# Layer 3's first product of the second-last quad moved among the last quad's norms, and the first quad worked out plainly ahead of the pairs

## The chip, the core and the metric

The kernel runs on one core of a Trainium2 chip. The metric is the device time of one execution in microseconds, the median of several runs; the kernel before takes 3154.85 us (three runs, 3150.97 to 3155.34). The profile is of one execution with a span of 3149.4 us. Engines are named as the profile names them: PE is TensorE's matmul side and PEld its weight loads, DVE is VectorE, ACT is ScalarE, POOL is GpSimd, SP is SyncE, which here only issues transfers.

## What is computed

Four residual graph layers with a layer norm after each, on x of shape 128 x 128 x 256 (graphs, nodes, features). Everything is float32.

```python
x = layernorm(x + L0(x))       # graph attention over 512 edges, 4 heads
x = layernorm(x + L1(x))       # three products by weights 256->512->1024->256, each mixed by adj*adj
x = layernorm(x + L2(x))       # three weights 256->256, mixed by diagonal, upper and lower part of adj
x = layernorm(x + L3(x))

def L3(features, A, W1, b1, g1, be1, W2, b2, g2, be2):
    A_hat = normalized(A + I)
    agg = einsum('nm,bmd->bnd', A_hat, features)
    h = relu(batchnorm(agg.reshape(-1, 256) @ W1.T + b1, g1, be1))   # 256 -> 512
    out = batchnorm(h @ W2.T + b2, g2, be2)                          # 512 -> 256
    return out
# batchnorm: mean and variance over ALL rows, that is, over all 128 graphs and 128 nodes
```

The two batch norms of layer 3 cut the computation in three. Nothing of the second product of layer 3 can begin before the first product has been done for every graph, and no output row is finished before the second product has been done for every graph.

## The kernel before

Graphs are handled in 32 quads of four, numbered 0 to 31. A first phase is a software pipeline: iteration k works on several quads at once, quad a = k - 1 in layers 2 and 3, quad c = k in layer 1, and later quads in layer 0. When a quad leaves it, two things have been stored to device memory: x3, the input of layer 3, and z, the first product of layer 3 (`hidden`), of which only the statistics are kept on the chip. The very last quad's z isn't stored: its norm's factors are known as soon as its statistics are, so it is normalized and passed through relu straight from PSUM (`hidden_last`).

The second phase loads z of all other quads, normalizes, applies relu, and multiplies by W2. The third phase adds x3 and does the last layer norm.

Many products are done two by two blocks at a time with seven block products in place of eight (class `Seven`, steps p1 to p7, with sums of blocks S1 to S4 of one operand and T1 to T4 of the other). The steps hang together through two PSUM banks y and z that are added to in turn:

```python
class Seven:
    def p1(self): self.y = ps("y"); self.mm(self.y, "A11", "B11", True);  self.k1 = self.part(self.y, 0)
    def p5(self): self.z = ps("z"); self.mm(self.z, "S1", "T1", True)
    def p2(self): x = ps("x");      self.mm(x, "A12", "B21", True);       self.out(0, 0, x, self.k1)
    def p6(self): self.mm(self.y, "S2", "T2", False);  self.k2 = self.part(self.y, 1)
    def p7(self): self.mm(self.y, "S3", "T3", False);  self.k3 = self.part(self.y, 2); self.out(1, 1, self.z, self.k3)
    def p4(self): self.mm(self.y, "A22", "T4", False); self.out(1, 0, self.y, None)
    def p3(self): self.mm(self.z, "S4", "B22", False); self.out(0, 1, self.z, self.k2)
# part: ScalarE copies the bank out.  out with a kept part: VectorE adds bank and part.
# out without one: ScalarE copies the bank.
```

The end of the first phase, for the last two quads:

```python
def stage_f(k):                       # agg, with A_hat, into SBUF
    pas = [ps("pa") for _ in range(DC)]
    for i0, dc in ((i0, dc) for i0 in range(0, QB, 2) for dc in range(DC)):
        for i in (i0, i0 + 1):
            nc.tensor.matmul(pas[dc][:, i * N:(i + 1) * N], s.xr[:, i, dc * P:(dc + 1) * P], ahat_t, ...)
    for dc, pa in enumerate(pas):
        nc.scalar.copy(ag[dc], pa)

def z_tile(k):                        # ONE buffer
    quads[k].zt = zpool.tile([P, K3, QB * N], F32, tag="z", name="z", bufs=1)

def hidden_stats(k):
    for c in range(K3):
        nc.vector.bn_stats(st1[:, c, k, :], zt[:, c, :])
    nc.sync.dma_start(z_dram[k], zt.rearrange("p c n -> p (c n)"))

def hidden_last(k, c):
    if c == 0:
        kept["z"] = z_tile(k)
    ...                               # two products 128x512 into ph
    nc.vector.bn_stats(st1[:, c, k, :], ph)
    batch_norm(st1, c, bn1, sc1, sh1, c)
    nc.scalar.activation(s.zt[:, c, :], ph, AF.Relu, bias=sh1[:, c:c + 1], scale=sc1[:, c:c + 1])

# iteration(31): a = 30, c = 31, nothing later
stage_f(30)
h = hidden(30, ...)
run(h.p1, h.p5); run(h.p2, h.p6); h.p7(); run(h.p4, h.p3)
hidden_stats(30)
for _ in third(31, 0): pass           # layer 1's third product, first two graphs
rest = third(31, 2); next(rest)
third_mix(31, 0); third_norm(31, 0)
for _ in rest: pass
third_mix(31, 2); third_norm(31, 2)
layer2(31, None): head(0), head(1), twelve of fourteen products
# iteration(32): a = 31
the rest of layer2(31): v.p4, v.p3, mixes, norms, store of x3
stage_f(31)
for i in range(K3): hidden_last(31, i)
```

The second phase takes quads in pairs, again with seven products, one pair's last two standing in the next pair. Two quads are left over and worked out plainly, with eight products of 128x512 each: quad 31, in front of the pairs, and quad 30, after them.

```python
nc.vector.tensor_add(s1, a21, a22)     # sums of W2's blocks: four of these
...
pairs = [begin(0)]                     # loads of z
for i in range(4): relus(pairs[0], i)
sums_of(pairs[0], 0)
plain(NQ - 1, load_z(NQ - 1), ...)     # quad 31, z is on the chip
for q in range(0, NQ - 2, 2):
    ...
    pair(pairs[d], pairs[d - 1] if d else None, next pair)
for c in range(K3): relu(z_last, c)
pair(None, pairs[-1], None)            # A22 product, then S4 product of the last pair
plain(NQ - 2, z_last, ..., True)       # quad 30, with the second batch norm in it
```

Of the kernel before, what the change touches and what calls it, by code (L numbers as in the profile page):

```python
# [8 lines left out]
F32 = mybir.dt.float32  # L9
# [17 lines left out]
def gnn_stack(ctx: ExitStack, tc: tile.TileContext, x, adj, w_qv_t, a, w_out_t, src, dst,  # L27
# [101 lines left out]
    with ExitStack() as phase:  # L129
# [76 lines left out]
            return t  # L206

        quads[0].xr = load_x(0)
        wqv = cload([P, DC, 2 * D], "wqv", w_qv_t.rearrange("(c p) f -> p c f", p=P))
        a_sb = cload([P, N], "adj", adj)  # L210
        a_bc = ctile([P, D], "a_bc", pool=cst)
        wt_t = ctile([P, N], "wt_t", pool=cst)
# [79 lines left out]

        def room_of(tag, n):

            t = {"m2": m2_tile, "adc": adc_tile}[tag]()
            return [t[:, i * 512:(i + 1) * 512] for i in range(n)]

        def queries(k, kept_at):
# [379 lines left out]
                s.xb = wk.tile([P, QB, D], F32, tag="xb", name=f"xb{k}", bufs=1)  # L678
            nc.gpsimd.tensor_add(s.xb[:, j:j + 2, :], xj, bias.unsqueeze(1).to_broadcast([P, 2, D]))  # L679

        def layer2(k, b):

            s = quads[k]
            adc = adc_tile()
            g = [wk.tile([P, 2, 3 * D], F32, tag="ms", name="g", bufs=1),
                 adc[:, :6 * D].rearrange("p (t f) -> p t f", t=2)]
            sums = [adc[:, 6 * D:], None]
            half = 3 * D // 2  # L690
# [91 lines left out]
            normed(1, mv)  # L782
            nc.sync.dma_start(x3_dram[k], s.xr.rearrange("p b d -> p (b d)"))

        def stage_f(k):

            s = quads[k]
            wide = wk.tile([P, DC, 3 * D], F32, tag="ms", name="ag", bufs=1)
            ag = [wide[:, i, :QB * N] for i in range(DC)]
            s.spare = [wide[:, i, QB * N:] for i in range(DC)]  # L790
            pas = [ps("pa") for _ in range(DC)]
            for i0, dc in ((i0, dc) for i0 in range(0, QB, 2) for dc in range(DC)):
                for i in (i0, i0 + 1):
                    nc.tensor.matmul(pas[dc][:, i * N:(i + 1) * N], s.xr[:, i, dc * P:(dc + 1) * P], ahat_t,
                                     start=True, stop=True)
            for dc, pa in enumerate(pas):
                nc.scalar.copy(ag[dc], pa)
            s.ag = ag

        def hidden_sums():  # L800

            blocks = {f"A{o + 1}{h + 1}": l3w1[:, h, o * 256:(o + 1) * 256] for o in range(2) for h in range(2)}
            for i in range(4):
                blocks[f"S{i + 1}"] = l3w1_s[:, i]
            sums_a(blocks, blocks)
            hidden.blocks = blocks

        def z_tile(k):
            quads[k].zt = zpool.tile([P, K3, QB * N], F32, tag="z", name="z", bufs=1)
# [73 lines left out]
        def run(*parts):  # L883
            for p in parts:
                p()

        def iteration(k):
# [5 lines left out]
                late_sums(c)  # L893
            parts = quads[a].layer2
            if not has_c:
                for _ in parts:
                    pass
            steps = softmax_parts(e) if has_e else iter(())
            if has_c:
                between = {i: [] for i in range(14)}  # L900
# [21 lines left out]
            if has_g:  # L922
                q = queries(g, room[:3])
            stage_f(a)
            if not has_c:
                for i in range(K3):
                    hidden_last(a, i)
                return
            h = hidden(a, room[5:] + room[2:4])
            if has_g:  # L930
# [25 lines left out]
                attention(e)  # L956
                scatter(e)
            rest = third(c, 2)
            if not has_b:
                next(rest)  # L960
                third_mix(c, 0)
                third_norm(c, 0)
                for _ in rest:
                    pass
                third_mix(c, 2)
                third_norm(c, 2)
                quads[c].layer2 = layer2(c, None)
                next(quads[c].layer2)
                next(quads[c].layer2)
                return  # L970
            mix1(b, 0)
            mix1(b, 2)
            third_mix(c, 0)
# [303 lines left out]
    with ExitStack() as phase:  # L1277
# [37 lines left out]
        with tc.manual_schedule(engines=None):  # L1315

            ws_ = ctile([P, 4, 2, P], "l3w2_s", pool=cst)
            a11, a12, a21, a22 = (w2t[:, 2 * h:2 * h + 2, o * P:(o + 1) * P] for o in range(2) for h in range(2))  # L1320
            s1, s2, s3, s4 = (ws_[:, i] for i in range(4))

# [8 lines left out]
            def plain(q, z, jobs, last=False):  # L1331
                ag = out_tile(q)
                po = [ps("po3") for _ in range(DC)]
                for o, c in jobs:
                    nc.tensor.matmul(po[o], w2t[:, c, o * P:(o + 1) * P], z[c // 2][:, c % 2, :],
                                     start=(c == 0), stop=(c == K3 - 1))
                for o in range(DC):
                    nc.vector.bn_stats(st2[:, o, q, :], po[o])
                    if last:
                        batch_norm(st2, o, bn2, sc2, sh2, K3 + o)  # L1340
                        halves(0, o, outs[0])
                        spread(o)
                    nc.vector.tensor_copy(ag[:, o, :], po[o])

            class Pair:
# [46 lines left out]
                    for c in (0, 1):  # L1392
                        relu(d.z[i % 2], 2 * (i // 2) + c)

            def pair(d, old, new):
# [12 lines left out]
                if d:  # L1408
                    sums_of(d, 3)
                    product(d.zb, s1, d.t[0], True)  # L1410
# [18 lines left out]
            nc.vector.tensor_add(s1, a21, a22)  # L1429
            nc.vector.tensor_sub(s2, s1, a11)  # L1430
            nc.vector.tensor_sub(s3, a11, a21)
            nc.vector.tensor_sub(s4, a12, s2)
            pairs = [begin(0)]
            for i in range(4):
                relus(pairs[0], i)
            sums_of(pairs[0], 0)

            plain(NQ - 1, load_z(NQ - 1), [(o, c) for c in range(K3) for o in range(DC)])
            for q in range(0, NQ - 2, 2):
                if q + 2 < NQ - 2:  # L1440
                    pairs.append(begin(q + 2))
                else:
                    z_last = load_z(NQ - 2)
                d, n = q // 2, len(pairs)
                pair(pairs[d], pairs[d - 1] if d else None, pairs[d + 1] if d + 1 < n else None)
            for c in range(K3):
                relu(z_last, c)
            pair(None, pairs[-1], None)
            plain(NQ - 2, z_last, [(o, c) for o in range(DC) for c in range(K3)], True)

            x3s, sums, mvs, coefs = {}, {}, {}, {}

# [123 lines left out]
```

## Time and profile before

| | |
|---|---|
| median of three runs | 3154.85 us |
| span of the profiled execution | 3149.4 us |
| busy: PE, PEld, DVE, ACT, POOL | 3077.0, 2403.3, 2306.6, 1376.0, 651.5 us |
| mean granted TensorE clock | 0.993 |
| moved by DMA | 340.04 MB, 108 GB/s over the span |
| first phase, up to quad 31's leaving it | to about 2825 us |
| batch norm and plain products of quad 31 | to about 2841 us |
| pairs | to about 3028 us |
| plain products of quad 30 and second batch norm | to about 3039 us |
| third phase | to the end |

How to read it: the busy time of PE over the whole span says little about this change, because the change touches only the place where one phase gives way to the next. There the engines run short of work and wait for one another, and the question is which wait ends last at each step. Three views answer it: busy time by stretches of time, the waits of PE within a stretch, and the timeline, which gives the start of each group of instructions and in brackets the idle time before it with what ended it. A product of this kernel shows as several records[...].

### The profile page before, as it was taken

The numbers are of one execution on the slowest core, as the hardware profiler recorded it, in microseconds if no ns is written. First come the engines' busy times: TensorE is split into PE (matmuls) and PEld (weight loads), VectorE is DVE, ScalarE is ACT, GpSimd is POOL, SyncE is SP. The second block draws the span as 40 slices with busy tenths as digits, with TensorE's granted clock in tenths as the row PEclk, the third lists the DMA queues.
The fourth block names the chain that finished last, engine by engine and source line by source line (L and its number), as shares of the span: only waits on it lengthen the run. The fifth ranks groups of instructions, "written<-read, shape, count | busy, mean of one in ns | idle before, by whom it ended". The sixth has DMA issues, their size and how long they took to land. (4 is left out here: it accounts for less than half of the span.)

```text
span 3149.4 us, 39744 instructions
## 1 busy us (share of the span) xinstructions
PE 3077.0 (98%) x14752; PEld 2403.3 (76%) x14752; DVE 2306.6 (73%) x4600; ACT 1376.0 (44%) x2548; POOL 651.5 (21%) x535
## 2 busy tenths in 40 slices
PE   7899999999999999999999999999999999989998
PEld 3678888888888888888888888888888887864444
DVE  7777777777777777777777777777777776447888
ACT  3344433444444444334344444444444344326668
POOL 2311222222121111122222211111122220001235
PEclk8999999999999999999999999999999999999999
DMA  5623333333333332333333333332333331005557
GB/s 179 160 68 88 101 108 97 106 108 108 101 86 103 104 91 79 98 108 101 101 108 108 103 94 92 107 91 76 97 108 101 101 108 41 21 31 195 173 195 275
DMA packets 117473, 340.04 MB, mean 108 GB/s; under 512 B 14881, under 2 KB 51617, under 8 KB 108961
## 3 DMA queue, kind: packets, MB, share of 16 engines
q0 software_dynamic: 44544, 147.88, 19.4%
q1 hardware_dynamic: 70976, 188.71, 17.0%
q8 instruction: 117, 1.92, 0.3%
q10 hardware_dynamic: 1760, 0.92, 0.1%
q14 instruction: 76, 0.61, 0.1%
HBM read 252.00 MB, written 85.46 MB: 107 GB/s over the span
## 5 line engine op out<-in xcount | busy, mean ns | idle before, releaser
L575 PE MATMUL ph<-m,w 128*128 128x256 f32 x2048 | 475.0, 380 | 0.0
L655 PE MATMUL p<-w,h 128*128 128x256 f32 x2048 | 463.8, 380 | 0.0
L575 PEld LDWEIGHTS ph<-m,w 128*128 128x128 f32 x2048 | 387.9, 191 | 78.4 <-issue 14.8
L655 PEld LDWEIGHTS p<-w,h 128*128 128x128 f32 x2048 | 389.7, 190 | 67.0 <-issue 8.1
L336 POOL DMA_INDIRECT zs<-qd,src_idx x120 | 117.2, 977 | 1347.8 <-DMA qd<-qt 1216.1
L575 PE MATMUL ph<-m,w_s 128*128 128x256 f32 x1536 | 357.5, 379 | 0.0
L575 PEld LDWEIGHTS ph<-m,w_s 128*128 128x128 f32 x1536 | 291.8, 190 | 52.9 <-issue 14.8
L336 POOL DMA_INDIRECT zs<-qd,dst_idx x120 | 188.1, 1568 | 352.5 <-DMA zs<-qd,src_idx 327.2
L581 ACT COPY u<-ph 128x512 f32<-128x512 f32 x128 | 74.8, 584 | 356.1 <-PE ph L575 356.1
L418 POOL DMA_INDIRECT attd<-at,att_idx x128 | 142.7, 1115 | 347.4 <-DMA attd<-at,att_idx 245.0
L591 ACT ACTIVATE h<-h 128x512 f32<-128x512 f32 x192 | 121.1, 630 | 135.6 <-DVE h L587 135.6
L113 ACT ACTIVATE ln_sd<-ln_mv,eps 128x2 f32<-128x2 f32 x192 | 55.9, 291 | 281.6 <-DVE ln_mv L108 277.8
L370 DVE TENSOR_TENSOR zs<-zs,a_bc 128x1024 f32<-128x1024 f32 x125 | 153.1, 1225 | 4.3
L371 DVE TENSOR_REDUCE scores<-zs 128x16 f32<-128x1024 f32 x125 | 152.5, 1220 | 4.3
L718 ACT COPY x2k<-y 128x384 f32<-128x384 f32 x192 | 92.0, 479 | 138.3 <-PE y L711 113.8
L368 DVE SCALAR_TENSOR_TENSOR zs<-zs 128x1024 f32<-128x1024 f32 x125 | 151.4, 1211 | 0.1
L106 DVE BATCH_NORM_STATS2 ln_st<-xr 128x6 f32<-128x256 f32 x384 | 144.5, 418 | 6.6
L121 DVE TENSOR_SCALAR xr<-xr,ln_mv,ln_rs 128x256 f32<-128x256 f32 x384 | 143.2, 415 | 7.0
L587 DVE TENSOR_TENSOR h<-ph,u 128x512 f32<-128x512 f32 x128 | 87.1, 680 | 73.1 <-PE ph L575 55.0
L437 ACT COPY adc<-ad 128x512 f32<-128x512 f32 x125 | 133.1, 1065 | 4.1 <-DMA ad<-attd 4.1
L679 POOL TENSOR_TENSOR xb<-xr,bias 128x512 f32<-128x512 f32 x64 | 99.3, 1551 | 160.0 <-DVE xr L121 150.7
L532 PE MATMUL pm<-wt_t,h 128*128 128x128 f32 x1024 | 126.7, 277 | 0.0
(342 smaller groups left out, 6071.1 us busy)
## 6 DMA issues: line engine op xcount, KB each, us to landing
ad<-attd SPq DMA_DIRECT2D x32, 1024.0 KB, 4.8
zd<-z SPq DMA_DIRECT2D x31, 1024.0 KB, 7.3
zl<-zd SPq DMA_DIRECT2D x62, 512.0 KB, 3.8
xr<-in_x_dram SPq DMA_DIRECT2D x32, 512.0 KB, 7.5
x3d<-xr SPq DMA_DIRECT2D x32, 512.0 KB, 2.6
x3l<-x3d SPq DMA_DIRECT2D x32, 512.0 KB, 5.1
out_dram<-x3l POOLq DMA_DIRECT2D x31, 512.0 KB
qd<-qt SPq DMA_DIRECT2D x30, 512.0 KB, 2.6
```

Source lines behind the costliest of these rows:

```text
L106: nc.vector.bn_stats(st[:, i, :], r[:, i, :])
L121: nc.vector.tensor_scalar(r[:, i, :], r[:, i, :], mv[:, i, 0:1], rs[:, i:i + 1], op0=ALU.subtract, op1=ALU.mult)
L336: nc.gpsimd.indirect_dma_start(out=s.z[c], out_offset=None, in_=s.qd, in_offset=bass.IndirectOffsetOnAxis(ap=idx[:, c:c + 1], axis=0), com ...
L368: nc.vector.scalar_tensor_tensor(z, z, SLOPE, z, op0=ALU.mult, op1=ALU.max)
L370: nc.vector.tensor_mul(z3, z3, a_bc.unsqueeze(1).to_broadcast([P, QB, D]))
L371: nc.vector.reduce_sum(s.es[:, c, :], z.rearrange("p (r d) -> p r d", d=DH), axis=AX.X)
L418: nc.gpsimd.indirect_dma_start(out=ad, out_offset=bass.IndirectOffsetOnAxis(ap=att_idx[:, c:c + 1], axis=0), in_=s.at[:, c, :], in_offset= ...
L437: (copy or nc.scalar.copy)(s.adc[:, j * H:(j + 1) * H, :], s.ad.rearrange("p (s r) -> p r s", r=R)[:, j * H:(j + 1) * H, :])
L532: nc.tensor.matmul(pm[:, c // 2, c % 2, :], quads[k].h1[i, c], wt_t, start=True, stop=True)
L575: nc.tensor.matmul(bank[g][:, i].rearrange("p b n -> p (b n)"), wa[:, c, f:f + P], s.m2[:, blk_b, c].rearrange("p b n -> p (b n)"), start= ...
L591: nc.scalar.activation(h, h if src_ is None else src_, AF.Relu)
L655: nc.tensor.matmul(p3[:, t * D:(t + 1) * D], s.h2[f // 2][:, f % 2, j + t, :], w3_sb[:, f, :], start=(f == 0), stop=(f == K2 - 1))
```

## The change

The first product of layer 3 for quad 30 is no longer done in one block ahead of quad 31's norms. Its seven steps are spread out: p1, p5 and p2 stand at the places where PE waited for the norms of layer 1 of quad 31, p6 and p7 among the products and norms of layer 2, p4 and p3 in the middle of `stage_f(31)`. The aim is that PE has a product to do while a norm runs on VectorE and ScalarE, and that the norms themselves begin earlier. To make room, the first half of layer 2's results for quad 31 is kept in the buffer m2 in place of ms, which still holds quad 30's aggregate. The sums of W2's blocks are made earlier too (`last_sums`), in the buffer that held layer 0's weights, which moves to another pool for that.

In the second phase the quad that is worked out plainly with stored z is quad 0 and no longer quad 30. Its products stand in front of the pairs, which now begin at quad 1 and end at quad 30. They are meant to give PE work while ScalarE and VectorE prepare the first pair. After the last pair there is now only that pair's end, with the S4 product ahead of the A22 product, and the second batch norm within it.

```diff
-        wqv = cload([P, DC, 2 * D], "wqv", ...)
+        wqv = cload([P, DC, 2 * D], "wqv", ..., pool=xpool)
...
-        def layer2(k, b):
+        def layer2(k, b, room=None):
...
-            g = [wk.tile([P, 2, 3 * D], F32, tag="ms", name="g", bufs=1),
+            g = [wk.tile([P, 2, 3 * D], F32, tag="ms", name="g", bufs=1) if room is None else room,
...
-        def stage_f(k):
+        def stage_f(k, amid=None):
...
+                if i0 and dc == 0 and amid:
+                    amid()
...
+        def last_sums():
+            kept["w2s"] = xpool.tile([P, 4, 2, P], F32, tag="wqv", name="l3w2_s", bufs=1)
+            ...
+            sums_a(a, {f"S{i + 1}": kept["w2s"][:, i] for i in range(4)})
...
 # iteration(32), a = 31
+                h = quads[a - 1].hidden
+                h.p6()
+                for _ in range(4):
+                    next(parts)
+                next(parts)
+                h.p7()
                 for _ in parts:
                     pass
+                def amid():
+                    run(h.p4, h.p3)
+                    hidden_stats(a - 1)
+                stage_f(a, amid)
+                for i in range(K3):
+                    hidden_last(a, i)
+                return
...
 # iteration(31), a = 30, c = 31
+                last_sums()
+                h = quads[a].hidden = hidden(a, room[5:] + room[3:5])
+                for _ in third(c, 0):
+                    pass
+                rest = third(c, 2)
+                next(rest)
+                third_mix(c, 0)
+                third_norm(c, 0)
+                for _ in rest:
+                    pass
+                h.p1()
+                third_mix(c, 2)
+                third_norm(c, 2)
+                lower = kept["m2"][:, :3 * 512].rearrange("p (t f) -> p t f", t=2)
+                quads[c].layer2 = layer2(c, None, lower)
+                next(quads[c].layer2)
+                run(h.p5, h.p2)
+                next(quads[c].layer2)
                 return
...
 # second phase
+            def finish(d):
+                product(d.zb, s4, d.b22, False)
+                result(d, 0, 1, d.zb, d.u2)
+                product(d.y, a22, d.t[3], False)
+                norm_over(0)
+                nc.vector.bn_stats(st2[:, 1, d.q, :], d.y)
+                norm_over(1)
+                nc.scalar.copy(outs[d.q][:, 1, :], d.y)
...
-            pairs = [begin(0)]
+            z_first = load_z(0)
+            pairs = [begin(1)]
+            for _ in plain(NQ - 1, load_z(NQ - 1)):
+                pass
+            for c in range(K3):
+                relu(z_first, c)
+            first_quad = plain(0, z_first)
+            next(first_quad)                    # the products; statistics and copies later, in the first pair
             for i in range(4):
                 relus(pairs[0], i)
-            sums_of(pairs[0], 0)
-            plain(NQ - 1, load_z(NQ - 1), ...)
-            for q in range(0, NQ - 2, 2):
+                if i == 1:
+                    sums_of(pairs[0], 0)
+            for q in range(1, NQ - 1, 2):
...
-            for c in range(K3):
-                relu(z_last, c)
-            pair(None, pairs[-1], None)
-            plain(NQ - 2, z_last, ..., True)
+            finish(pairs[-1])
```

More of the change, by code (lines that the diff above doesn't have):

```diff
@@ L208, in gnn_stack @@
         quads[0].xr = load_x(0)
[L209 removed]
+        wqv = cload([P, DC, 2 * D], "wqv", w_qv_t.rearrange("(c p) f -> p c f", p=P), pool=xpool)
         a_sb = cload([P, N], "adj", adj)
@@ L293, in room_of @@
         def room_of(tag, n):
-            t = {"m2": m2_tile, "adc": adc_tile}[tag]()
+            t = kept[tag] = {"m2": m2_tile, "adc": adc_tile}[tag]()
             return [t[:, i * 512:(i + 1) * 512] for i in range(n)]
@@ L806, in hidden_sums @@
             hidden.blocks = blocks
+        def last_sums():
+            kept["w2s"] = xpool.tile([P, 4, 2, P], F32, tag="wqv", name="l3w2_s", bufs=1)
+            a = {f"A{o + 1}{h + 1}": kept["w2t"][:, 2 * h:2 * h + 2, o * P:(o + 1) * P] for o in range(2)
+                 for h in range(2)}
+            sums_a(a, {f"S{i + 1}": kept["w2s"][:, i] for i in range(4)})
         def z_tile(k):
@@ L924, in iteration @@
             stage_f(a)
-            if not has_c:
-                for i in range(K3):
-                    hidden_last(a, i)
+            if not has_b:
+                last_sums()
[16 more added lines that the diff above has]
+                next(quads[c].layer2)
                 return
@@ L958, in iteration @@
             rest = third(c, 2)
[L959 to L970, printed above, removed]
             mix1(b, 0)
@@ L1315, in gnn_stack @@
         with tc.manual_schedule(engines=None):
-            ws_ = ctile([P, 4, 2, P], "l3w2_s", pool=cst)
+            ws_ = kept["w2s"]
             a11, a12, a21, a22 = (w2t[:, 2 * h:2 * h + 2, o * P:(o + 1) * P] for o in range(2) for h in range(2))
@@ L1329, in out_tile, with plain @@
                 return outs[q]
-            def plain(q, z, jobs, last=False):
+            def plain(q, z):
                 ag = out_tile(q)
                 po = [ps("po3") for _ in range(DC)]
-                for o, c in jobs:
+                for o, c in ((o, c) for c in range(K3) for o in range(DC)):
                     nc.tensor.matmul(po[o], w2t[:, c, o * P:(o + 1) * P], z[c // 2][:, c % 2, :],
                                      start=(c == 0), stop=(c == K3 - 1))
+                yield
                 for o in range(DC):
                     nc.vector.bn_stats(st2[:, o, q, :], po[o])
[L1339 to L1342, printed above, removed]
                     nc.vector.tensor_copy(ag[:, o, :], po[o])
@@ L1393, in relus, with pair @@
                         relu(d.z[i % 2], 2 * (i // 2) + c)
-            def pair(d, old, new):
+            def pair(d, old, new, rest=()):
                 if d:
@@ L1409, in pair @@
                     sums_of(d, 3)
+                    for _ in rest:
+                        pass
                     product(d.zb, s1, d.t[0], True)
@@ L1427, in pair, with norm_over @@
                     relus(new, 3)
[L1429 to L1432, printed above, removed]
-            pairs = [begin(0)]
+            def norm_over(o):
+                batch_norm(st2, o, bn2, sc2, sh2, K3 + o)
+                halves(0, o, outs[0])
+                spread(o)
+            def finish(d):
[9 more added lines that the diff above has]
+            for _ in plain(NQ - 1, load_z(NQ - 1)):
+                pass
+            for c in range(K3):
+                relu(z_first, c)
+            first_quad = plain(0, z_first)
+            next(first_quad)
             for i in range(4):
                 relus(pairs[0], i)
-            sums_of(pairs[0], 0)
-            plain(NQ - 1, load_z(NQ - 1), [(o, c) for c in range(K3) for o in range(DC)])
-            for q in range(0, NQ - 2, 2):
-                if q + 2 < NQ - 2:
+                if i == 1:
+                    sums_of(pairs[0], 0)
+            for q in range(1, NQ - 1, 2):
+                if q + 2 < NQ - 1:
                     pairs.append(begin(q + 2))
-                else:
-                    z_last = load_z(NQ - 2)
                 d, n = q // 2, len(pairs)
-                pair(pairs[d], pairs[d - 1] if d else None, pairs[d + 1] if d + 1 < n else None)
-            for c in range(K3):
-                relu(z_last, c)
-            pair(None, pairs[-1], None)
-            plain(NQ - 2, z_last, [(o, c) for o in range(DC) for c in range(K3)], True)
+                pair(pairs[d], pairs[d - 1] if d else None, pairs[d + 1] if d + 1 < n else None, first_quad)
+            finish(pairs[-1])
             x3s, sums, mvs, coefs = {}, {}, {}, {}
```

## The prediction, made before the changed kernel had been run

> **What bounds the kernel now.** I read the totals and slices of the page first, then a table of busy time by stage over the last fifth of the span, then TensorE's waits in that part, and last the timeline there.
>
> ```profile
> PE 3077.0 (98%) x14752; PEld 2403.3 (76%) x14752; DVE 2306.6 (73%) x4600; ACT 1376.0 (44%) x2548; POOL 651.5 (21%) x535
> PE   7899999999999999999999999999999999989998
> ```
>
> TensorE (PE) is busy 98% of the span. The second line shows where it isn't: at the very start, and in the last six slices. Table by stage (stretch, length, then busy time and count of PE, weight loads, VectorE, ScalarE, GpSimd, then PE clock, DMA share, GB/s):
>
> ```profile
> 2695.20:2775.20 80.00, 78.85 (x394) 64.14 (x393) 39.34 (x96) 26.11 (x51) 2.57 (x2) 1.00 0.05 20
> 2775.20:2785.90 10.70, 8.88 (x46) 6.94 (x45) 3.68 (x7) 4.03 (x7) 0.00 (x0) 1.00 0.01 2
> 2785.90:2805.50 19.60, 16.39 (x74) 13.18 (x73) 8.15 (x21) 2.24 (x5) 1.27 (x1) 1.00 0.13 54
> 2805.50:2824.90 19.40, 15.88 (x56) 9.04 (x56) 12.53 (x33) 5.62 (x13) 1.28 (x1) 1.00 0.03 10
> 2824.90:2841.30 16.40, 14.39 (x33) 6.04 (x34) 10.84 (x28) 6.64 (x12) 0.00 (x0) 1.00 0.53 185
> 2841.30:2852.10 10.80, 7.19 (x14) 2.78 (x13) 7.58 (x7) 5.64 (x9) 2.35 (x1) 0.84 0.65 238
> 2852.10:3020.30 168.20, 168.20 (x394) 74.45 (x392) 137.83 (x140) 109.00 (x166) 33.94 (x14) 1.00 0.53 172
> ```
>
> Up to 2775 a quad takes 80 us with no hole, and from 2852 fourteen pairs take 12.02 us each with none. Between them, 2775 to 2852, the pipeline drains and refills: layer 3's first product of quad 30 alone (2775 to 2786), the norms and layer 2 of quad 31 (to 2825), the batch norm (to 2841), the first pair (to 2852). After 3039 ScalarE sets the pace (97.0 of 110.5 us). The change touches the seam and the end of the pairs. The waits of PE in the seam (line waiting, releaser: us in total, times, longest):
>
> ```profile
> PE y L1374 <- DVE t L1366: 3.2, 1, 3.2
> PE pa L794 <- DVE xr L121: 2.7, 2, 1.6
> PE pt L697 <- DVE xr L121: 2.5, 1, 2.5
> PE po L1335 <- ACT z L857: 2.0, 2, 1.1
> PE y L823 <- ACT m L827: 1.4, 2, 0.7
> ```
>
> The waits view leaves out about 0.2 us at each wait, because it counts a matmul's drain as busy. So I counted from start to start in the timeline against what products cost with no wait: a product of hidden 0.86 us (4 records), a layer-2 product 0.65, a 128x512 product 0.86 (two passes of 0.43), a pair's product 1.72.
> - 2775.2 to 2785.9: needs 1.7 + 7 x 0.86 = 7.8 of 10.7; lost 2.9.
> - to 2805.5: third's 32 products at 0.43, two mixes at 0.86, a transpose group 0.43: 16.0 of 19.6; lost 3.6.
> - to 2824.9: 0.4 + 14 x 0.65 + 3.4 + 1.7 = 14.6 of 19.5; lost 4.8.
> - to 2841.3: 16 x 0.86 = 13.7 of 16.4; lost 2.7.
> - to 2852.1: 3 x 1.72 = 5.2 of 10.8; lost 5.6, of which 1.6 is the clock.
> Together **19.6 us** of PE time is lost in the seam.
>
> **What the Trainium skill says.** "TensorE: Matmul & The Clock Gate", section "What's actually happening": TensorE falls to half clock after an idle window of about 3.4 us and needs a busy one to recover. The trace agrees: after the 3.2 us wait the next four records take 0.86 each in place of 0.43, while the wait of 2.5 us at 2805 costs nothing afterwards.
>
> ```profile
> 2848.75 3.48 PE L1374 MATMUL y<-t,l3w_s 128*128 128x512 f32 x4 [3.23 <-DVE t L1366]
> ```
>
> "SBUF — State Buffer", section "Who interferes with whom": a VectorE instruction with two SBUF inputs contends with a GpSimd one that reads SBUF. The trace agrees: the subtraction L1366 takes 2.8 to 3.2 us beside GpSimd's L1368, where L1364, with the same shape, takes 1.23. "DMA: Bandwidth & Descriptors", section "Anatomy of one DMA — SWDGE (gpsimd) path": fixed 2.0 us plus bytes over 436 GB/s, which would make 1 MB an estimated 4.4 us; that section is of the other queue, and the trace has 3.8 to 7.8 us from issue to landing for z, so I use the trace.
>
> **The change, part by part.** No PE work is added or removed: the order of instructions shows the same products, with quad 0 in place of quad 30 as the one worked out plainly. What moves is order, so the sum is a walk along the three in-order queues with the durations above, from 2775.17, where both kernels are alike.
> 1. *Hidden(30) taken out of its place.* Third starts at 2776.9 in place of 2785.9. Its first mix is at 2785.5, its last product ends at 2791.6.
> 2. *Among the norms.* p1 (0.86) covers the copy of s3 (0.9 lost before). The second mix starts at 2792.5; the transposes of its norm come 4.04 later as before (2801.42 to 2805.46), at 2796.5; the first transposes, p5 and p2 fill that to 2795.5: 1.0 lost in place of 2.6. The twelve layer-2 products end at 2804.8. p6 covers the 0.7 ahead of the thirteenth. The mixes run from 2807.1 to 2810.5. The last quad's first norm is ready 4.64 after they start, at 2811.7; p7 fills to 2811.4: 0.3 lost in place of 1.2.
> 3. *Amid stage f.* Four transposes to 2812.6, p4 to 2813.4. p3 must wait for VectorE to add p7's part to z, which stands in its queue behind the second norm's statistics: 2814.1 (0.7 lost); then the other four to 2815.9. Before, the second norm cost 2.0 here. The copies of ag release the plain products at 2816.55, against 2824.93.
> 4. *The batch norm.* VectorE must add p3's part and take the four statistics of quad 30 (0.7 + 2.5 us) before the first statistics of quad 31: from 2815.2 to 2818.4, just when these are due (2.0 us after the first product: 2818.6). Each of the four rounds then costs 2.64; the subtractions for layer 3's second weights, which stretched two rounds to 3.4 and 2.8 before, now stand at 2775 where VectorE is idle. Last shift at 2829.2, 12.65 after the first product, against 13.67.
> 5. *z's store.* Quad 31's z goes into the one z buffer, so its first relu waits until quad 30's store has landed. The store can start at 2815.9, lands 3.8 us later if undisturbed (before, it began at 2786.8 and moved its data by 2790.2), and the relu is due at 2821.6. I take it as hidden.
> 6. *Quad 0 plainly.* The loads start when the last plain product of hidden is done, as before: 2823.7. Products of quad 31 wait for its relus: 1.9 lost in two places, as 2.4 before; they end at 2832.1. Then quad 0's eight (6.85) run to 2838.9, while ScalarE does the eight relus of the first pair (5.7 us), and VectorE its two differences by 2841.1, due at 2842.3. So the waits of 0.5 and 3.5 and the slow clock (1.6) go.
> The pairs start at 2838.9 with one plain quad more behind them. Before, the first pair began as if at 2852.07 - 3 x 1.72 = 2846.9. The gain of the front is 2846.9 + 6.85 - 2838.9 = **14.9 us**.
> 7. *The end.* Before, plain(30) covered the last pair's norm. From the last S3 product at 3022.02 to the transposes that wait for the second shift took 16.9 us:
>
> ```profile
> 3038.91 0.44 PE L1466 MATMUL pt<-ident,agg 128*128 128x128 f32 x2 [3.32 <-ACT agg L1308]
> ```
>
> Now: product ends 3023.8, copy and add to 3025.3, S4 product to 3027.2, add and statistics (1.4) to 3028.6, the first batch norm with its two spreads to 3031.0, statistics of y 0.7, second batch norm to 3033.8, scaling 0.6: 3034.45. That is 12.4, and 6.85 went to the front: **2.4 us given back**.
> Net 14.9 - 2.4 = 12.5. A walk like this misses semaphore delays, so I take 1 us off: 11.5 of 3154.85, which is 3143.4.
>
> **Rivals.**
> - *The one z buffer becomes the wait.* The store now leaves about 1 us after quad 31's x3 store, which shares its queue. With the longest landing in the trace (7.8) the relu would start at 2823.7, two late, and ScalarE's queue would pass most of that on through the roots of the next rounds. For it: 1.5 MB leave in a row. Against it: nothing else moves then (10 GB/s in that stretch). Time 3145.5.
> - *VectorE becomes the bound of the seam.* Step 4 leaves it no slack: each delay of p3 delays all four rounds. If the layer-2 additions run late by the 0.7 us addition of p2's part, put in ahead of the sums for layer 2, the whole seam slips by up to 1.5. Time 3145.
> - *The loads come too late.* Six loads in place of four must land before the first pair's second difference, 3.1 MB from 2823.7; at the 238 GB/s of the table that is 2836.9, with the lead-in about 2839, due for relu at 2837. One relu of quad 0 now also stands in ScalarE's queue ahead of quad 31's last one. Costs up to 3 us. Time 3146.
> - *The end gives back more*, if TensorE, idle from 3028.7, runs the first quads of the last stage at half clock for longer; it already did so before (0.95 over that stage). Below 1 us.
>
> **Range and chances.** The seam can't give more than the 19.6 lost, so with nothing given back 3135 is the floor; two of the rivals together make 3148.5. The runs of before spread by 4.4 us, which is part of the range. 3138 to 3149.5. Two per cent is 63 us, more than everything lost between 2775 and 3039, so within 2% is all but sure.
>
> **What would show it.** PE's waits between the last full quad and the first pair add up to some 4 us in place of 14; no half clock at the first pair; S4 ahead of A22 at the end and a longer chain there. A wait of the first z relu on a DMA, or a first statistics of quad 31 held up by VectorE, would show the rivals. Wrong altogether I would be if the loads or a buffer stall the pairs in their steady state, beyond 12.02 us each.

## The result, and the profile after

The changed kernel takes **3139.41 us** (median of four runs, 3137.62 to 3142.95), against 3154.8 us for the kernel before (four runs, 3150.97 to 3155.34): a ratio of 0.9955, 95% interval 0.9938 to 0.9972, or 15 us less. The profiled execution has a span of 3135.9 us against 3149.4.

Totals and slices of the page, after:

```profile
PE 3070.0 (98%) x14752; PEld 2399.9 (77%) x14752; DVE 2307.2 (74%) x4600; ACT 1375.0 (44%) x2548; POOL 649.8 (21%) x535
PE   7899999999999999999999999999999999999987
```

The same 14752 matmul records, and the slice that holds the seam, the fifth from the end, is now a 9 where it was an 8. The last two slices have each lost a tenth, because the third phase, where TensorE isn't the bound, begins earlier and fills more of them. TensorE's waits between quad 30's stage f and the first pairs, after (line waiting, releaser: us in total, times, longest):

```profile
PE po L1364 <- ACT z L866: 1.3, 2, 1.0
PE pt L697 <- DVE xr L121: 0.7, 1, 0.7
PE z L832 <- DVE z L845: 0.4, 1, 0.4
PE ph L862 <- ACT ag L799: 0.2, 1, 0.2
PE pa L796 <- DVE xr L121: 0.2, 1, 0.2
```

They add up to 2.8 us, where the same view of the kernel before adds up to 14.2. The 3.2 us at the first pair are gone, the two waits for the last quad's norms have shrunk from 2.7 to 0.2, the one for layer 1's second norm from 2.5 to 0.7. The timeline of TensorE through the seam shows what stands there now (start, length, line, op, out<-in, idle time before and its releaser in brackets; lines between those shown are left out):

```profile
2773.93 1.95 PE L796 MATMUL pa<-ahat_t,xr 128*128 128x128 f32 x16
2790.39 1.03 PE L832 MATMUL y<-ag,l3w 128*128 128x256 f32 x4
2795.32 0.67 PE L697 MATMUL pt<-ident,xr 128*128 128x128 f32 x4 [0.74 <-DVE xr L121]
2809.26 1.03 PE L832 MATMUL y<-m,l3w_s 128*128 128x256 f32 x4
2810.47 1.26 PE L796 MATMUL pa<-ahat_t,xr 128*128 128x128 f32 x8 [0.18 <-DVE xr L121]
2812.97 1.13 PE L832 MATMUL z<-ag,l3w_s 128*128 128x256 f32 x4 [0.37 <-DVE z L845]
2815.22 7.13 PE L862 MATMUL ph<-ag,l3w 128*128 128x512 f32 x16 [0.23 <-ACT ag L799]
2830.90 7.03 PE L1364 MATMUL po<-zl,l3w 128*128 128x512 f32 x16
2837.77 1.88 PE L1400 MATMUL y<-zl,l3w 128*128 128x512 f32 x4
2839.48 1.88 PE L1400 MATMUL z<-t,l3w_s 128*128 128x512 f32 x4
2841.20 1.88 PE L1400 MATMUL y<-t,l3w_s 128*128 128x512 f32 x4
2842.92 1.88 PE L1400 MATMUL x3p<-zl,l3w 128*128 128x512 f32 x4
```

Of quad 30's steps, p1 (2790.39) covers a copy of ScalarE that cost 0.7 us before, p7 (2809.26) and p3 (2812.97) stand among the last quad's norms. Quad 0's plain products (L1364 from `zl`, 2830.90) run into the first pair, and the three products of the first pair follow one another at 1.72 us with no wait and no slow clock.

The starts before, from which the next table counts, in TensorE's timeline (the transposes at 3038.91 are shown in the prediction):

```profile
2775.17 1.95 PE L794 MATMUL pa<-ahat_t,xr 128*128 128x128 f32 x16
2824.93 7.13 PE L853 MATMUL ph<-ag,l3w 128*128 128x512 f32 x16 [0.28 <-ACT ag L797]
2841.28 1.88 PE L1374 MATMUL y<-zl,l3w 128*128 128x512 f32 x4
2852.07 1.88 PE L1374 MATMUL x3p<-zl,l3w 128*128 128x512 f32 x4
3022.02 1.88 PE L1374 MATMUL y<-t,l3w_s 128*128 128x512 f32 x4
```

Counted from the start of quad 30's stage f (2775.17 before, 2773.93 after), with "transposes" for the pair that waits for the second batch norm's last shift (the first row is a part of the second, and "together" adds up rows two to five; the last S3 product and the transposes after the change, at 3012.87 and 3025.47, are shown further down):

| | before, us | after, us | difference |
|---|---|---|---|
| stage f of quad 30 to quad 31's plain products | 49.76 | 41.29 | 8.47 |
| to the first product of the first pair | 66.11 | 63.84, of which 6.85 quad 0 | 9.12 |
| from there to the first pair's x3p product | 10.79 | 5.15 | 5.64 |
| from there to the last S3 product | 169.95 | 169.95 | 0 |
| from there to the transposes | 16.89 | 12.60 | 4.29, less 6.85 for the quad moved: -2.56 |
| together | | | **12.20** |
| up to stage f of quad 30 | 2775.17 | 2773.93 | 1.24 |
| from the transposes to the end | 110.49 | 110.43 | 0.06 |

Twelve of the 13.5 us between the two profiles lie where the change is. The 1.24 ahead of it is the start of the kernel, which the change does not touch apart from a buffer: over all the kernels below with the changed first phase, stage f of quad 30 starts anywhere between 2773.92 and 2779.02.

### The profile page after: what moved, and what is told of

It reads as the page before. It is cut to its first block, busy times and chain, and to the rows that moved or that the text cites. A ratio compares the mean times of both kernels' runs of the same rounds, so it can differ in the third digit from the quotient of the medians.

```text
span 3135.9 us, 39741 instructions
## 1 busy us (share of the span) xinstructions
PE 3070.0 (98%) x14752; PEld 2399.9 (77%) x14752; DVE 2307.2 (74%) x4600; ACT 1375.0 (44%) x2548; POOL 649.8 (21%) x535
```

## Experiments

**Each half alone.** First, the changed first phase with the second phase of before (quad 31 plain in front, quad 30 after the pairs); then the reverse, with the sums of W2 back in the second phase too.

```diff
 # first half alone: second phase of before
-            pairs = [begin(1)]
+            pairs = [begin(0)]
-            first_quad = plain(0, z_first)
-            finish(pairs[-1])
+            pair(None, pairs[-1], None)
+            plain(NQ - 2, z_last, ..., True)
 # second half alone: first phase of before
-                last_sums()
-                h.p1() ... run(h.p5, h.p2) ... h.p6() ... h.p7() ... amid()
+                h = hidden(30); run(h.p1, h.p5); run(h.p2, h.p6); h.p7(); run(h.p4, h.p3); hidden_stats(30)
```

> The first half of the change alone: the seven products of quad 30 spread out and the sums of W2 made early, but quad 31 plain in front of the pairs and quad 30 plain after them, as before. Theory (the two halves add up, and most of the gain is made ahead of the plain products): quad 31's plain products start 41.3 us after quad 30's stage f begins, as in the changed kernel; the first pair then waits some 3 us for its relus and differences, which nothing covers, perhaps with 1.6 us of half clock; its first difference is multiplied about 63 us after the start of stage f. The front gains 9 to 12 us over the kernel before, the end stays at 16.9 us, the whole is 9 to 12 us faster than before, so that the second half is worth only 1 to 3 us on top. Rival (what is gained ahead is given back at the first pair, because VectorE and ScalarE are as late as before): under 7 us faster.

> The second half of the change alone: quad 0 plain in front of the pairs and the short end, but quad 30's hidden in its old place and the sums of W2 in the second phase. Theory: the waits of 0.5 and 3.5 us and the 1.6 us of half clock at the first pair go, 5.6 us; 2.4 to 2.6 are given back at the end (12.5 in place of 16.9 us, with 6.85 us moved): 3 us faster than before. Rival (the gain of the change is in the plain quad's place): over 7 us faster. Rival (the end gives everything back): 0.

Measured: the first half alone 3148.27 us against 3155.63 (ratio 0.9971, 0.9960 to 0.9982), 7.4 us less; the second half alone 3152.39 (0.9990, 0.9984 to 0.9997), 3.2 us less. By stages, with the front counted without the moved quad:

| gain over before, us | ahead of the pairs | in the first pair and behind it | end | to the transposes |
|---|---|---|---|---|
| first half alone | 9.11 | -0.65 | -0.01 | 8.45 |
| second half alone | -1.70 | 5.64 | -2.56 | 1.38 |
| both (the change) | 9.12 | 5.64 | -2.56 | 12.20 |

TensorE at the first pair, first half alone:

```profile
2831.10 1.88 PE L1403 MATMUL y<-zl,l3w 128*128 128x512 f32 x4
2837.86 3.75 PE L1403 MATMUL y<-t,l3w_s 128*128 128x512 f32 x4 [3.17 <-DVE t L1395]
2841.41 3.01 PE L1403 MATMUL x3p<-zl,l3w 128*128 128x512 f32 x4
2844.26 1.88 PE L1403 MATMUL y<-t,l3w_s 128*128 128x512 f32 x4
```

All that the spread steps gain ahead of the pairs arrives there (2831.10 is 57.00 after stage f, as 63.84 - 6.85 = 56.99 in the changed kernel). But the first pair still waits 3.2 us for VectorE's difference, and then the clock is halved over two products: from start to start 3.55 and 2.85 us in place of 1.72, 2.96 us more, where the kernel before lost 1.6. So this half lies between the two expectations: its gain is not eaten at the first pair, but at 8.45 us in the trace it is smaller than the 9 to 12 us of the theory, by the longer slow stretch (1.36 us). Quad 0's products take these losses away, 5.64 us counted from the kernel before (rows two and three), 6.3 on top of the first half. The 1.70 us that the second half seems to lose ahead of the pairs are one slow stretch of the clock as well; in the timeline of that kernel the first plain products of quad 31 (sixteen records) take 8.81 us in place of 7.13, although the waits ahead of them are those of before:

```profile
2823.15 1.26 PE L794 MATMUL pa<-ahat_t,xr 128*128 128x128 f32 x8 [1.64 <-DVE xr L121]
2824.69 8.81 PE L853 MATMUL ph<-ag,l3w 128*128 128x512 f32 x16 [0.28 <-ACT ag L797]
```

Without it the second half gives 5.64 - 2.56 = 3.1, which is what was expected and what its time shows. By stages, with the first half's slow stretch at the pair set aside too, the two halves add up: 9.11 + 5.64 - 2.56 = 12.19. By times they don't quite: 7.4 + 3.2 = 10.6 us, against 15 for the whole change. The slow stretches and the third phases of these two profiles, which are longer than before by 3.6 and 2.0 us, go in that direction; that they make up the difference is not shown.

**VectorE between the last norm and the batch norm.** Quad 30's four statistics twice, and not at all. These two and the next were single runs, read from their traces alone:

```diff
-            for c in range(K3):
-                nc.vector.bn_stats(st1[:, c, k, :], zt[:, c, :])
+            for _ in range(2 if k == NQ - 2 else 1):        # twice
+                for c in range(K3):
+                    nc.vector.bn_stats(st1[:, c, k, :], zt[:, c, :])
+            # not at all, for k == NQ - 2 (quad 29's are used in their place):
+            nc.gpsimd.tensor_copy(st1[:, :, k, :], st1[:, :, k - 1, :])
```

> The changed kernel with quad 30's four statistics taken twice, 2.4 us more for VectorE ahead of quad 31's first statistics. Theory (VectorE has no slack there, so each microsecond ahead of the first statistics delays all four rounds): the first statistics of quad 31 start 4.4 us after its first plain product in place of 2.03, the last shift 15.0 us after it in place of 12.66, and the first pair begins 2.2 to 2.5 us later counted from quad 30's stage f. Rival (z's store or TensorE set the start of the rounds): below 0.5 us later.

> The changed kernel without quad 30's four statistics (GpSimd copies those of quad 29 into their place, so the output differs slightly), 2.4 us less for VectorE. Theory (VectorE's statistics and TensorE's first product are ready within 0.1 us of one another, so taking one away gives nothing): first statistics of quad 31 still 1.9 to 2.03 us after its first plain product, the first pair at most 0.2 us earlier. Rival (VectorE alone is the bound): up to 1.2 us earlier, as far as z's store allows, which has 1.2 us to spare.

VectorE's timeline around quad 31's first statistics, in the changed kernel, then with the statistics twice, then without:

```profile
2814.86 2.47 DVE L852 BATCH_NORM_STATS2 st<-z 128x6 f32<-128x512 f32 x4
2817.25 0.69 DVE L864 BATCH_NORM_STATS2 st<-ph 128x6 f32<-128x512 f32 x1
```

```profile
2816.80 4.84 DVE L853 BATCH_NORM_STATS2 st<-z 128x6 f32<-128x512 f32 x8
2821.55 0.68 DVE L865 BATCH_NORM_STATS2 st<-ph 128x6 f32<-128x512 f32 x1
```

```profile
2822.33 0.70 DVE L867 BATCH_NORM_STATS2 st<-ph 128x6 f32<-128x512 f32 x1 [2.41 <-PE ph L865]
```

The first plain product starts at 2815.22, 2817.15 and 2820.31 in the three, so the first statistics come 2.03, 4.40 and 2.02 us after it. Doubling delays the last shift from 12.66 to 15.03 us after that product and the first pair by 2.04; leaving the statistics out brings nothing (0.06 later). Without them VectorE is idle for 2.4 us and waits for TensorE's product: the two paths meet there. Of the delay of 2.37 at the last shift 0.33 is missing at the pair. In the changed kernel, as ScalarE's timeline shows, one relu of quad 0 stands ahead of quad 31's last one:

```profile
2827.55 0.81 ACT L1354 ACTIVATE zl<-zl,sh,sc 128x512 f32<-128x512 f32 x1 [0.31 <-ACT bn_t L93]
2828.27 0.76 ACT L866 ACTIVATE z<-ph,sh,sc 128x512 f32<-128x512 f32 x1
```

The shift is there at 2827.88, the relu starts 0.39 later; with a later shift ScalarE has done the relus of quad 0 before it.

**The sums of W2 back in the rounds of the batch norm.**

```diff
-                last_sums()
...
-            ws_ = kept["w2s"]
+            ws_ = ctile([P, 4, 2, P], "l3w2_s", pool=cst)
+            nc.vector.tensor_add(s1, a21, a22)              # and three subtractions
```

> The changed kernel with the sums of W2's blocks back in the second phase, among the rounds of the batch norm. Theory (they stretch the rounds as they did before): last shift 13.6 to 13.8 us after the first plain product in place of 12.66, the first pair 0.8 to 1.1 us later counted from quad 30's stage f. VectorE's work in front of layer 2 gets no shorter, since the sums stood where it was idle. Rival (VectorE has the time between two rounds' steps): below 0.3 us.

The first pair comes 0.28 us later, the last shift 13.26 us after the first product. So the rival is nearer in size, though not in its reason. All four now fall into one round, the third, between steps that wait for each other, and lengthen it from 2.64 to 3.25; in the kernel before they fell into two (3.45 for the third, and 2.92 from the last statistics to the end of the last shift, where 2.72 is usual). Of that 0.6, 0.3 is taken up by the same relu as above. Making the sums early is worth 0.3 us of the twelve.

**The end: A22 ahead of S4.**

```diff
             def finish(d):
+                product(d.y, a22, d.t[3], False)
+                nc.vector.bn_stats(st2[:, 1, d.q, :], d.y)
                 product(d.zb, s4, d.b22, False)
+                norm_over(1)
                 result(d, 0, 1, d.zb, d.u2)
-                product(d.y, a22, d.t[3], False)
                 norm_over(0)
-                nc.vector.bn_stats(st2[:, 1, d.q, :], d.y)
-                norm_over(1)
```

> The changed kernel with the last pair's two closing products in the other order: the A22 product and its batch norm first, then S4, and the first output's batch norm last. Theory (the end is a chain of PE, VectorE and spreads that begins with a wait of 1.4 us for VectorE's z): A22 needs only the bank y and fills that wait, the first batch norm runs during S4, one norm remains after it: 11.2 to 11.6 us from the last S3 product to the last transposes in place of 12.6, so 1.0 to 1.4 us faster than the changed kernel. Rival (two batch norms behind one another set the end, whichever comes first): 12.4 to 12.8 us, no gain.

TensorE's timeline at the end, first of the changed kernel, then with A22 first (L1510 makes the shift's row, L1515 begins the scaling):

```profile
3012.87 1.88 PE L1400 MATMUL y<-t,l3w_s 128*128 128x512 f32 x4
3016.15 1.98 PE L1400 MATMUL z<-zl,l3w_s 128*128 128x512 f32 x4 [1.40 <-DVE agg L1413]
3017.97 1.88 PE L1400 MATMUL y<-t,l3w 128*128 128x512 f32 x4
3025.47 0.69 PE L1507 MATMUL pt<-ident,agg 128*128 128x128 f32 x2 [2.72 <-ACT agg L1337]
```

```profile
3015.88 1.88 PE L1400 MATMUL y<-t,l3w_s 128*128 128x512 f32 x4
3018.44 1.98 PE L1400 MATMUL y<-t,l3w 128*128 128x512 f32 x4 [0.68 <-ACT u L1405]
3020.26 1.88 PE L1400 MATMUL z<-zl,l3w_s 128*128 128x512 f32 x4
3027.76 1.12 PE L1507 MATMUL pt<-ident,agg 128*128 128x128 f32 x4 [5.62 <-ACT agg L1337]
```

In the changed kernel the transposes start 12.60 us after the last S3 product, with A22 first 11.88: 0.72 gained, not 1.0 to 1.4. But now four transposes wait there in place of two, at half clock (0.23 us each from start to start, in place of 0.11 in the seam), so that the scaling starts only 0.3 us earlier (13.64 against 13.93). VectorE sets this end. The first and last of a run of its instructions, in the changed kernel and then with A22 first:

```profile
3018.17 0.69 DVE L1413 TENSOR_TENSOR agg<-z,u 128x512 f32<-128x512 f32 x1 [1.35 <-PE z L1400]
3024.56 0.22 DVE L97 SCALAR_TENSOR_TENSOR sh<-bn_t,sc,bn 128x1 f32<-128x1 f32 x1
```

```profile
3020.46 0.70 DVE L1465 BATCH_NORM_STATS2 st<-y 128x6 f32<-128x512 f32 x1 [0.62 <-PE y L1400]
3026.85 0.22 DVE L97 SCALAR_TENSOR_TENSOR sh<-bn_t,sc,bn 128x1 f32<-128x1 f32 x1
```

It works without a wait from the addition after S4 to the last shift in the changed kernel (3018.17 to 3024.78), and from the statistics after A22 to the last shift in the other order (3020.46 to 3027.07). That is 6.61 us both times, and the other order only lets it begin 0.72 earlier. Its time, 3141.39 us (0.9950, 0.9936 to 0.9964), can't be told from the changed kernel's.

**Half of a quad as cover.** One output row of quad 30 in front, the other at the end; its z is loaded twice for that, and A22 stands first as above:

```diff
-            z_first = load_z(0)
-            pairs = [begin(1)]
-            first_quad = plain(0, z_first)
+            z_first = load_z(NQ - 2)
+            pairs = [begin(0)]
+            first_quad = plain(NQ - 2, z_first, (0,))       # first output row only
 # finish: A22 and its statistics, S4, then the second row of quad 30, norm_over(0), norm_over(1)
```

> The changed kernel with the plain quad cut in two: of quad 30 only the first output row (four products, 3.43 us) stands in front of the pairs, the other row (3.43 us) at the end, between the last pair's A22 and S4 products' norms; the pairs begin at quad 0. Theory (the first pair needs only about half of the 6.85 us of cover, and the end has room for the other half): the front is 3.1 to 3.4 us shorter than in the changed kernel, with a wait of at most 0.5 us for the first pair's second difference, the end 12.8 to 13.4 us in place of 12.6: 2.3 to 3 us faster than the changed kernel. Rival (the first pair needs the whole cover): its first difference comes 2 to 3 us late, and the time is that of the changed kernel within 1 us.

TensorE at the first pair, with half of a quad in front:

```profile
2834.38 1.88 PE L1400 MATMUL y<-zl,l3w 128*128 128x512 f32 x4
2836.10 1.88 PE L1400 MATMUL z<-t,l3w_s 128*128 128x512 f32 x4
2838.24 1.95 PE L1400 MATMUL y<-t,l3w_s 128*128 128x512 f32 x4 [0.26 <-DVE t L1392]
```

As the theory has it, half of the cover is all but enough: the second difference is 0.4 us late from start to start (2.14 in place of 1.72). The front is 2.93 us shorter, a little less than the 3.1 to 3.4 expected, and the end takes 13.59 us in place of 12.60, a little more than the 12.8 to 13.4, which leaves 1.94. Yet the time is 3141.53 us (0.9955, 0.9942 to 0.9969), no better than the changed kernel's. In this profile the third phase, counted from its first scaling products, takes 114.8 us in place of 109.1.

**The third phase.** That difference had to be explained before the times could be compared. ScalarE sets the pace there, and over the first six profiles its waits for `nm` (minus the mean times the reciprocal `rs`, which VectorE makes for the last layer norm) go roughly with the length of the phase: 4.1 us before (109.7 us), 3.5 after (109.1), 6.7 with the first half alone (113.3), 5.0 with the second (111.7), 3.1 with A22 first (110.2), 8.8 with half a quad (114.8). One of them in the timeline of the last kernel, four lines of VectorE, GpSimd and ScalarE:

```profile
3107.38 0.77 POOL L1564 DMA_DIRECT2D out_dram<-x3l  x1 [0.99 <-POOL x3l L1523]
3107.60 1.88 DVE L1546 SCALAR_TENSOR_TENSOR nm<-mv,rs 128x4 f32<-128x4 f32 x1
3108.17 1.27 POOL L1523 TENSOR_TENSOR x3l<-x3l,shift_bc 128x512 f32<-128x512 f32 x1
3109.51 1.09 ACT L1558 ACTIVATE x3l<-x3l,nm,rs 128x256 f32<-128x256 f32 x2 [1.51 <-DVE nm L1546]
```

A product of 128 x 4 elements, 0.16 us elsewhere, takes 1.88 and ends when GpSimd's addition ends (3109.48 and 3109.44). In the six profiles 18 of the 192 products that make `nm` take 0.65 us or more, and each of them ends within 0.05 us of the end of one of these additions. The product has two inputs in SBUF. The test takes one of them to PSUM, in the kernel before, the changed one and the one with half a quad:

```diff
+                rp = ps("rp3")[:, :QB]                      # PSUM
+                nc.vector.reciprocal(rp, coefs[q])
+                nc.vector.scalar_tensor_tensor(nm, mvs[q][:, :, 0], -1.0, rp, op0=ALU.mult, op1=ALU.mult)
                 nc.vector.reciprocal(rs, coefs[q])          # SBUF, as before
-                nc.vector.scalar_tensor_tensor(nm, mvs[q][:, :, 0], -1.0, rs, op0=ALU.mult, op1=ALU.mult)
```

> The kernel before, with one edit in the third phase: the product that makes nm reads the reciprocal from PSUM in place of SBUF (a second reciprocal of 0.14 us is added for it), so that no VectorE instruction of the third phase has two inputs in SBUF. Theory (the third phase differs from run to run because a VectorE instruction with two SBUF inputs now and then waits until GpSimd's addition has ended, 1.3 to 1.9 us in place of 0.16, and ScalarE, which sets the pace, waits for it): no nm longer than 0.3 us, ScalarE's waits for nm at most 0.8 us in all in place of 4.1, the time 2 to 5 us below the kernel before, and runs closer together. Rival (the long nm is only where another wait, of GpSimd's stores or of the loads, is seen): the waits move to another instruction, and the time stays within 1 us.

> The changed kernel with the same edit in the third phase. Theory: no long nm; third phase 105.5 to 107 us from its first scaling products to the end in place of 109.1; the distance to the kernel before with the same edit is what the traces give for the seam and the end of the pairs, 12.2 us (11 to 13.5). Rival (the change itself shortens or lengthens the third phase through its loads): the distance is off that by more than 2 us.

> The kernel with half of quad 30 in front of the pairs and half at the end, with the same edit in the third phase. Theory (its path to the third phase is 2.6 us shorter than the changed kernel's, which its time did not show because its third phase had more long nm, 8.8 us of ScalarE's waits in place of 3.5): 2 to 3 us faster than the changed kernel with this edit. Rival (the shorter path is given back in the third phase in another way, because x3's loads come later): within 0.7 us of it.

The tile `nm` in the kernel before without the edit, and in the changed kernel with it (durations in ns, min/median/max):

```profile
L1494 DVE SCALAR_TENSOR_TENSOR nm<-mv,rs x32: 161/163/1911, 3046.2 to 3143.5; 128x4 f32<-128x4 f32 x32
```

```profile
L1536 DVE SCALAR_TENSOR_TENSOR nm<-mv,rp x32: 157/158/159, 3036.4 to 3131.8; 128x4 f32<-128x4 f32 x32
```

No long one is left in any of the three. Waits of ScalarE for `rs`, which is now made after `nm`, of 1.4 to 2.1 us in all have come instead, so a part of the rival holds, and the phase takes 108.1, 107.8 and 107.0 us in the three; for the changed kernel that is a little above the 105.5 to 107 expected. Times, on one chip with a kernel before at 3153.38:

| with the edit | median, us (runs) | ratio to before |
|---|---|---|
| kernel before | 3150.65 (3149.49 to 3155.73) | 0.9989 (0.9981 to 0.9998) |
| changed kernel | 3137.98 (3136.91 to 3139.41) | 0.9948 (0.9934 to 0.9961) |
| half a quad | **3135.59** (3134.80 to 3137.08) | 0.9942 (0.9928 to 0.9955) |

The kernel before gains 2.7 us by the edit, within the 2 to 5 expected, and its runs lie within 6.2 us in place of 9.1 (13 and 17 runs). With the third phase quieted, the change is worth 12.7 us, against 12.2 from the stages of the first two profiles. In the profiles of these two kernels, though, the same stages differ by 13.6 us, because in this execution the kernel before ran at half clock in quad 31's plain products as well:

```profile
2825.91 8.37 PE L853 MATMUL ph<-ag,l3w 128*128 128x512 f32 x16
```

That is 1.23 us more from start to start than in its first profile, with the same instructions up to there. So what the seam gives differs by more than a microsecond from one execution to the next. None of the eight profiles that have both halves of the change (seven of them with a further edit) shows a slow product between quad 30's stage f and the first pair's products, and each of the four others does.

Half a quad, with A22 first, is now 2.4 us ahead of the changed kernel (only one of its five runs is slower than the changed kernel's fastest), and 1.96 by the traces up to the transposes: the shorter path had been there. That last kernel is faster than both the kernel before and the changed one.

## Why the prediction was right

1. *Hidden(30) out of its place*: the second mix's and the transposes' places came as walked. The second transposes start 21.39 us after stage f (walked 21.33), the last quad's first norm is ready 36.54 after it (36.53).
2. *Among the norms*: 0.7 us lost ahead of the second transposes, as the profile counts, in place of 1.0; 0.2 at the first norm. The extra addition ahead of layer 2's sums cost 0.04 us at one layer-2 product, so that half of the VectorE rival did not come.
3. *Amid stage f*: p3 waits for VectorE's addition, 0.54 from start to start (0.7 walked). The plain products start 41.29 after stage f (41.38).
4. *The batch norm*: last shift 12.66 after the first product (12.65), and VectorE has no slack; doubling the statistics shows it. Leaving them out gains nothing, because TensorE's first product is ready at the same moment. The place where the step was off is the sums: in the kernel before they do lengthen the rounds by the whole microsecond between 13.67 and 12.65 (0.81 and 0.20), but left in their place in the changed kernel they cost only 0.6 at the shift and 0.3 at the pair.
5. *z's store*: issued at 2814.90 and landed in 3.9 us, the first relu came at 2820.05 and waited for VectorE's shift. 1.2 us were to spare, so the one-buffer rival did not come. That was read from one trace; the store was not held back in an experiment.

The store, in the DMA view of that stretch (KB, then us from issue to landing):

```profile
zd<-z SPq DMA_DIRECT2D x1, 1024.0 KB, 3.9
```

6. *Quad 0 plainly*: the first pair starts 63.84 after stage f (63.73), with no wait and no slow clock; the front gains 14.76 (14.9). The rival of late loads came in one of its two parts: a relu of quad 0 stood ahead of quad 31's last one and cost about 0.3 us. The loads caused no wait of TensorE.
7. *The end*: 12.60 (12.4), 2.56 given back (2.4). The fourth rival came in small: the clock is halved already at those transposes, and from them to the first scaling products it takes 1.33 us in place of 0.77.

The signs that it named came too: waits of 2.8 us where it gave some 4, no half clock at the first pair, a longer chain at the end, and 169.95 us from the first pair's x3p product to the last S3 product, as before.

The sum of the steps, 12.5, is 0.3 off the 12.2 of the first two profiles and 0.2 off the 12.7 of the pair with the quieted third phase. So close an agreement is partly luck, since the seam of the kernel before differed by 1.4 us between its two profiles. The step that failed is the last one: *a walk like this misses semaphore delays, so I take 1 us off.* The durations had been taken from start to start and held those delays already.

The predicted 3143.4 us is 4.0 above the measured median. The failed step is 1.0 of it, and the steps' sum 0.2. The other 2.7, between 12.7 and the 15.4 of the medians, are not shown to be part of the seam: the third phase of single profiles varies by over 5 us with the collisions above, and the start by 5. None of this was a term of the sum; only the 4.4 us by which the runs of before spread stood for it in the range. That the median fell inside the range, 1.4 us from its lower end, is therefore partly luck, and one of the four runs, 3137.62, lies below it.

## What to carry to other kernels

Where one phase drained into the next, a walk from start to start along the in-order queues gave the gain of the stages to a few tenths of a microsecond, with nothing to be taken off for semaphores. It didn't give the stretches of slow clock, which differ by a microsecond or more between executions. Two pieces of cover, one for the norms and one for the first pair, added up by stages; but how much cover a gap needs is to be read there (half a quad did for a gap that a whole quad was put into), and what is moved away is missed where it stood. Before the times of variants that differ by 2 us are compared, look whether a later phase, the same in all, differs by more.

## What was not expected of the hardware

- A tiny VectorE instruction with two SBUF inputs can wait out GpSimd's work beside it: 0.65 to 1.95 us in place of 0.16, two to five times in the third phase of each of the first six profiles, at places that differ from kernel to kernel. "SBUF — State Buffer", section "Who interferes with whom" of the Trainium skill states that a VectorE instruction with two SBUF inputs contends with a GpSimd one that reads SBUF, and the trace agrees. That 4 elements per partition lose up to 1.8 us, as much as 1024 do (L1366, 2.81 and 3.17 us in place of 1.23), and that ScalarE, which sets the pace, then waits, only the trace showed. In the example above the product had begun 0.57 us before the addition, while GpSimd issued a store; why it didn't end first is not shown. With one input in PSUM all 32 took 0.157 to 0.159 us.
- TensorE's clock does not follow the length of one wait. After waits of 3.23 and 3.17 us at the same place in two kernels, 1.6 and 2.96 us were lost. After waits of 1.05 and 1.64 us the plain products of quad 31 ran at full clock in the first profile of the kernel before, and lost 1.68 us with the second half alone and 1.23 in the kernel before with the edit in the third phase. The prediction saw agreement with the idle window of about 3.4 us that it cites, in one wait of 3.2 us. These figures do not fit that rule, and the measurements decide. What sets the clock here is open.
